# One planner for the whole kernel: the first part of a macaron block ordered by the list scheduler, with smaller units, earlier scores and movable copies

## The chip, the cores and the metric

The kernel runs on one core of a Trainium2 chip. The core has a matrix engine (TensorE, in the profile PE, with its weight loads as PEld), a vector engine (VectorE, DVE), an activation engine (ScalarE, ACT), a general engine (GpSimd, POOL) and a queue engine (SyncE, SP). Each works through its own list of instructions in order and waits for the others by semaphores. SP, ACT and POOL also start transfers (DMA), which 16 DMA engines carry out. Indirect transfers, which scatter rows to addresses held in memory, are started by POOL.

The metric is the device time of one execution in microseconds (us). Lower is better.

## The reference

The input is 8 sequences of 256 tokens of 128 numbers. Three residual steps are computed on it:

```python
x = x + 0.5 * ffn(layernorm(x), router_w, w1, v1, w2, bias)
x = x + attention(layernorm(x), qkv_w, proj_w, proj_b, slopes)
x = x + 0.5 * ffn(layernorm(x), router_w, w1, v1, w2, bias)     # the same weights

def ffn(x, ...):                     # 8 experts, hidden width 352
    scores = softmax(x @ router_w)   # each token goes to its best two experts
    weights, idx = top_k(scores, 2)
    h = gelu(x @ w1[e]) * (x @ v1[e])
    y = h @ w2[e]
    return sum_k(weights[k] * y[idx[k]]) + bias

def attention(x, ...):               # 16 heads of 8, rotary turning of q and k
    s = q @ k.T * 8**-0.5 + min(j - i, 0) * slope[h] * 8
    return softmax(s) @ v @ proj_w.T + proj_b
```

All numbers are 32-bit floats.

## The kernel before

**First part.** The 2048 tokens are four blocks of 512 (two sequences each, four tiles of 128 tokens). For each block `ffn_prep` (line 634) normalises the rows (`ln_stats`, `ln_apply`; one step of the normalisation, a power, runs on POOL), turns them (`ln_turn`) and calls `route` (line 555). `route` multiplies by the router, finds the best two experts, counts with matmuls where each row goes among the rows of its expert, and has POOL scatter the rows to a buffer `xs` in HBM (line 621): one indirect transfer for 128 rows, eight for a block, 32 for a part. `wave` (line 659) makes a table of the 128-row tiles that are sure to be full so far: 8 tiles after two blocks, 16 after three, and all 39 after the fourth. In the last wave SP also writes blank rows behind each expert's last row (`pad`, line 677 to 681), eight transfers whose addresses it loads from the table `t_free`.

**Expert tiles.** The class `Tiles` (line 747) works off the table. For a tile, `load` (line 770) has SP fetch 128 rows into `xr` (10 buffers), `turn_x` transposes them, `weights` copies the expert's first weights to `ws`, `hidden` makes `g` and `v` (Gelu on ACT, product on DVE), and `second` multiplies by the other weights into `y`, scales it into `yo` (4 buffers) and has POOL scatter it to `ys` in HBM (line 836). A part always runs 36 tiles; three more stand behind a branch (`others`). In a step j, y of tile j - 3 comes before g and v of tile j - 1.

**Attention.** It runs in 32 groups n: 8 sequences times four groups of four heads (`group`, line 1009). A group has scores `s` on PE into four PSUM buffers; minima with bias on DVE (`ex`, `least`); Exp on ACT; transposes `eT` on PE; copies `et`, two on ACT and two on DVE; `o` on PE, then `og`, `ogT` and the division. `post1` reads the first part's results back and normalises them, `att_prep` makes q, k and v of a sequence, `after` projects. After every second sequence, `after` routes a block of the second part; the last wave of that part comes after the last block. The second part's expert tiles start when the last scores are done.

**What sets the order.** For attention and the second part an explicit planner, the class `Plan` (line 284), notes every operation with an engine, a duration, a due time and its needs, and `order` (line 351) places them as a list scheduler: at each step it takes the operation that can start first, by smaller due time among those that can start within 0.1 us. The instructions of PE, DVE, ACT and SP are then issued in that order; POOL's others are kept in it too, and its scatters stand behind the POOL operation ahead of them. The first part is not in the planner (`plan = None`, line 403): its instructions stand in the order of the text, and the framework orders each engine. Its loads are issued at the top: x on SP and ACT, weights `wall` on SP, six small tensors on ACT. `attention_constants` (line 171) spreads the preparation of attention over the first part's tiles. `behind` keeps two instructions of an engine in order. Between the parts the branch of `others` separates the two stretches of code.

Of the kernel before, what the change touches and what calls it, by code (L numbers as in the profile page):

```python
# [15 lines left out]
P = 128  # L16
# [21 lines left out]
def full_tiles(blocks):  # L38

    return (2 * TB * blocks - E * (P - 1)) // P  # L40
# [3 lines left out]
def tile_macaron(  # L44
# [30 lines left out]
    xs0 = []  # L75
    for b in range(NBLK):
        t = res.tile([P, TT, D], F32, tag=f"x0_{b}", name=f"x0_{b}")
        (nc.scalar if b % 2 else nc.sync).dma_start(
            t.rearrange("p (s t) d -> p s t d", t=2), xf[:, 2 * b : 2 * b + 2]
        )  # L80
        xs0.append(t)
    rw = const.tile([P, E], F32, name="rw")
    nc.scalar.dma_start(rw, router_w)
    wall = const.tile([P, E, WW], F32, name="wall")
    hb = const.tile([P, D], F32, name="hb")
    pb = const.tile([P, D], F32, name="pb")
    sl = const.tile([P, H], F32, name="sl")
    for e in range(E):
        nc.sync.dma_start(wall[:, e, 0:F], w1[e])
        nc.sync.dma_start(wall[:, e, F : 2 * F], v1[e])  # L90

    nc.vector.memset(wall[:16, :, 2 * F + D :], 0.0)
    for c, cut in enumerate(CUTS):
        skip = 16 if c else 0
        nc.sync.dma_start(
            wall[skip:, :, 2 * F + c * D : 2 * F + (c + 1) * D],
            w2[:, cut + skip : cut + P, :].rearrange("e p d -> p e d"),
        )
    qkvT = const.tile([P, 3 * D], F32, name="qkvT")
    pwT = const.tile([P, D], F32, name="pwT")  # L100
    cs = const.tile([P, 2, 2, 2, HD], F32, name="cs")
    nc.scalar.dma_start(sl, slopes.partition_broadcast(P))
    nc.scalar.dma_start(hb, bias.partition_broadcast(P))
    nc.scalar.dma_start(pb, proj_b.partition_broadcast(P))
    nc.scalar.dma_start(cs, rope.rearrange("(p n) a b d -> p n a b d", n=2))
    nc.scalar.dma_start(qkvT, qkv_wT)
    nc.scalar.dma_start(pwT, proj_wT)


    blank = const.tile([P, SPARE + E, RW], F32, name="blank")  # L110
    ident = const.tile([P, P], F32, name="ident")
    make_identity(nc, ident)
    half = const.tile([P, TT], F32, name="half")
    nc.vector.memset(half, -0.5)
    before = const.tile([P, P], F32, name="before")
    nc.gpsimd.memset(before, 1.0)
    nc.gpsimd.affine_select(
        out=before, in_=before, compare_op=ALU.is_gt, fill=0.0, base=0,
        pattern=[[1, P]], channel_multiplier=-1,
    )  # L120
    ones = const.tile([P, P], F32, name="ones")
    nc.gpsimd.memset(ones, 1.0)

    def counting(shape, pattern, name):
        cf = const.tile(shape, F32, name=name)
        ci = cf.bitcast(I32)
        nc.gpsimd.iota(ci, pattern=pattern, base=0, channel_multiplier=0)
        nc.vector.tensor_copy(cf, ci)
        return cf

    last_wave = NT - full_tiles(NBLK - 1)
    experts = counting([P, E], [[1, E]], "experts")
    regions = counting([P, E], [[REG, E]], "regions")

    rows = []
    for b in range(NBLK):
        t = const.tile([P, 2, TT, RW], F32, tag=f"rows{b}", name=f"rows{b}")
        for k in range(2):
            nc.gpsimd.iota(
                t[:, k, :, D : D + 1].bitcast(I32), pattern=[[SEQ, 2], [1, 2], [0, 1]],  # L140
                base=TOK * k + b * TB, channel_multiplier=2,
            )
        rows.append(t)
    steps128 = counting([P, E, 16], [[0, E], [P, 16]], "steps128")
    tiles = counting([P, last_wave, E], [[1, last_wave], [0, E]], "tiles")
    upto = const.tile([P, E, E], F32, name="upto")
    nc.gpsimd.memset(upto, 1.0)
    nc.gpsimd.affine_select(
        out=upto, in_=upto, compare_op=ALU.is_ge, fill=0.0, base=0,
        pattern=[[1, E], [-1, E]], channel_multiplier=0,  # L150
    )

    mask = const.tile([P, 4], F32, name="mask")

    vpad = [const.tile([P, 2, H, 32], F32, tag=f"vp{i}", name=f"vp{i}") for i in range(3)]


    strip = 3 * P
    alibi = const.tile([P, H, strip], F32, name="alibi")

    def behind(ins, other):

        tc.add_manual_dep(
            ins if isinstance(ins, mybir.Instruction) else ins.ins, other,
            mybir.DependencyInfo(
                mybir.DependencyClass.NoSync, mybir.DependencyReason.DATA
            ),
            reason="in the order of the text",
        )

    def attention_constants(other):


        def late(ins):
            behind(ins, other)

        late(nc.vector.tensor_scalar(hb, hb, 0.5, None, ALU.mult))
        late(nc.vector.tensor_reduce(
            mask, ident.rearrange("p (i j d) -> p j i d", j=4, d=HD), AX.XY, ALU.add
        ))  # L180
        yield
        for b in range(NBLK):
            late(keep(part0, b, xs0[b]))
            yield
        for t in vpad:
            late(nc.vector.memset(t, 0.0))
            late(nc.vector.memset(t[:, :, :, HD : HD + 1], 1.0))
            yield
        di = work.tile([P, 2 * SEQ], F32, tag="yg", name="di", bufs=4)[:, :strip].bitcast(I32)
        nc.gpsimd.iota(  # L190
            di.rearrange("p (a c) -> p a c", c=P), pattern=[[1, 3], [2, P]], base=-1,
            channel_multiplier=-2,
        )
        df = work.tile([P, 2 * SEQ], F32, tag="yg", name="df", bufs=4)[:, :strip]
        late(nc.vector.tensor_scalar(df, di, 0, None, ALU.min))
        yield
        for h in range(H):
            late(nc.vector.tensor_scalar(
                alibi[:, h, :], df, sl[:, h : h + 1], 8.0, ALU.mult, ALU.mult
            ))  # L200
            if h % 2:
                yield

    def run(gen):
        for _ in gen:
            pass


    ENG = mybir.EngineType
    PE, DVE, ACT, POOL, SP = ENG.PE, ENG.DVE, ENG.Activation, ENG.Pool, ENG.SP  # L210

    class Root:


        def __init__(self, make, slot=None, bufs=0, bank=False):
            self.make, self.slot, self.bufs, self.bank = make, slot, bufs, bank
            self.tile = None
            self.ops = []

        def real(self):  # L220
# [63 lines left out]
    class Plan:  # L284
# [7 lines left out]
        def note(self, eng, us, call, reads, writes, lands=0.0):  # L292
# [10 lines left out]
            for late, writing in [(x, False) for x in reads] + [(x, True) for x in writes]:  # L303
                root = late.root
                for other, region, wrote in root.ops:
                    if other is op:
                        continue
                    if root.bank and (other.eng is not eng or wrote != writing):
                        op.needs.add(other)
                    elif (wrote or writing) and meet(region, late.region):  # L310
                        op.needs.add(other)
# [923 lines left out]
```

## Time and profile before

| what | us |
|---|---|
| median of 3 runs | 463.69 (461.45 to 463.88) |
| the profiled execution itself | 498.11 |
| its span, first to last instruction | 496.4 |
| busy: PE / DVE / ACT / POOL | 383.7 / 310.2 / 269.6 / 247.2 |
| first row scatter of the first part begins | 21.5 |
| row scatters of the first part end | 70.9 |
| last y of the first part begins | 147.1 |
| first and last scores (groups 0 and 31) begin | 165.0 and 365.7 |
| last y scatter of the second part begins | 479.1 |

The profile is one execution recorded by the hardware profiler, some 34 us longer than the runs. In its lines an operation is named by line, engine and by what it writes and reads; `L415` and `L422` are the two lines of the helper through which nearly all operations pass, outside (`L415`) and inside the planner (`L422`). "Idle before" is the time for which an engine stood still ahead of an operation, and what ended that; "remote" means that the trace names nobody.

### The profile page before, as it was taken

To read this page: it belongs to the slowest core of one execution; us is meant where nothing else is said; L and a number is where in the kernel's file an instruction comes from. 1 tells how busy PE (TensorE), PEld (TensorE's weight loads), DVE (VectorE), ACT (ScalarE), POOL (GpSimd) and SP (SyncE) were. 2 spreads that over 40 slices of the span, in tenths; PEclk is the share of its full clock that TensorE was granted. 3 is DMA by queue.
4 is the path that set the end of the run, shared out by engine and by line. 5 is a ranking of instruction groups with operands and counts; after the bars stand their busy time and mean duration, and the time that the engine had idled before them with its cause. 6 is when DMAs were issued, how large, how long until landed. Compare 5 with 4: busy or idle time off the path is not lost. (4 is left out here: it accounts for less than half of the span.)

```text
span 496.4 us, 11146 instructions
## 1 busy us (share of the span) xinstructions
PE 383.7 (77%) x3272; PEld 310.6 (63%) x3272; DVE 310.2 (62%) x1300; ACT 269.6 (54%) x671; POOL 247.2 (50%) x324
## 2 busy tenths in 40 slices
PE   0643559999982788998999899788959984999950
PEld 0533449999981555656665566456636974899940
DVE  7332337874432697889888978698856671545514
ACT  2510214554540678888888797578847561445520
POOL 7273564554441136346948895638060546354430
PEclk9999988999996599999999999899997997999985
DMA  7971322222112110000000000010010112222116
GB/s 218 241 148 41 83 81 61 56 71 66 56 32 80 34 44 23 1 1 3 1 17 29 1 2 17 23 34 17 2 43 13 35 55 63 66 72 65 44 52 232
DMA packets 31646, 27.59 MB, mean 56 GB/s; under 512 B 4832, under 2 KB 29408, under 8 KB 31584
## 3 DMA queue, kind: packets, MB, share of 16 engines
q1 hardware_dynamic: 23760, 15.05, 11.7%
q0 software_dynamic: 4352, 8.99, 5.7%
q10 hardware_dynamic: 3472, 2.80, 1.7%
q8 instruction: 29, 0.48, 0.4%
q14 instruction: 33, 0.27, 0.2%
HBM read 14.80 MB, written 12.02 MB: 54 GB/s over the span
## 5 line engine op out<-in xcount | busy, mean ns | idle before, releaser
L422 ACT ACTIVATE ex<-ex,least 128x256 f32<-128x256 f32 x256 | 116.3, 504 | 21.6 <-DVE least L422 21.2
L836 POOL DMA_INDIRECT ys<-yo,xr x72 | 72.7, 1010 | 102.9 <-ACT yo L415 39.9
L422 DVE CUSTOM_DVE_ANT_0 ex<-s,alibi 128x256 f32<-128x256 f32 x256 | 96.0, 418 | 28.7 <-PE s L422 13.3
L621 POOL DMA_INDIRECT xs<-rows,r_at_f x64 | 63.1, 986 | 57.4 <-issue 15.7
L422 PE MATMUL eT<-ident,ex 128*128 128x128 f32 x512 | 78.4, 286 | 12.6 <-DVE et L422 7.5
L422 PEld LDWEIGHTS eT<-ident,ex 128*128 128x128 f32 x512 | 58.5, 145 | 35.2 <-ACT ex L422 24.8
L825 PE MATMUL y<-wall,gs 128*128 x432 | 62.9, 283 | 18.2 <-issue 8.9
L825 PEld LDWEIGHTS y<-wall,gs 128*128 128x128 f32 x432 | 55.4, 196 | 20.8 <-issue 9.6
L795 DVE COPY ws<-wall 128x704 f32 x72 | 38.4, 533 | 14.4 <-issue 7.4
L422 DVE COPY et<-eT 128x512 f32<-128x512 f32 x64 | 43.0, 684 | 2.6 <-remote 1.4
L422 PE MATMUL o<-et,vp 128*32 128x256 f32 x512 | 43.1, 400 | 0.8 <-DVE et L422 0.5
L422 DVE TENSOR_TENSOR gs<-gs,v 128x384 f32<-128x384 f32 x36 | 19.9, 553 | 36.8 <-PE xT L422 19.0
L422 ACT COPY et<-eT 128x512 f32<-128x512 f32 x64 | 36.5, 578 | 8.7 <-PE eT L422 7.6
L422 PE MATMUL s<-kT,qT 32*128 32x256 f32 x512 | 40.6, 419 | 0.6 <-DVE kT L422 0.6
L415 DVE TENSOR_TENSOR gs<-gs,v 128x384 f32<-128x384 f32 x36 | 19.8, 550 | 33.1 <-PE xT L415 14.1
L415 PE MATMUL g<-xTs,ws 128*128 128x128 f32 x216 | 32.1, 288 | 0.0
L422 PE MATMUL g<-xTs,ws 128*128 128x128 f32 x216 | 31.1, 281 | 0.6 <-DVE r_row_f L422 0.5
L415 PE MATMUL v<-xTs,ws 128*128 128x128 f32 x216 | 31.6, 284 | 0.0
L422 POOL TENSOR_SCALAR qT<-qa,mask 128x256 f32<-128x256 f32 x28 | 25.6, 928 | 10.9 <-ACT qa L422 10.8
L422 PEld LDWEIGHTS s<-kT,qT 32*128 32x128 f32 x512 | 25.7, 192 | 7.7 <-issue 4.6
L422 POOL TENSOR_TENSOR t<-qk,cs 128x128 f32<-128x128 f32 (+1 forms) x36 | 18.8, 550 | 23.2 <-ACT qk L422 23.1
L422 PE MATMUL v<-xTs,ws 128*128 128x128 f32 x216 | 30.3, 277 | 0.0
(219 smaller groups left out, 651.2 us busy)
## 6 DMA issues: line engine op xcount, KB each, us to landing
xr<-xs SPq DMA_DIRECT2D x72, 65.0 KB
yg<-ys SPq DMA_DIRECT2D x10, 256.0 KB
wall<-in_w_dram SPq DMA_DIRECT2D x8, 176.0 KB
wall<-in_v_dram SPq DMA_DIRECT2D x8, 176.0 KB
ys<-yo,xr POOLq DMA_INDIRECT x72
xs<-blank SPq DMA_DIRECT2D x16, 65.0 KB
xs<-rows,r_at_f POOLq DMA_INDIRECT x64
yg<-ys ACTq DMA_DIRECT2D x4, 256.0 KB
```

Of the source, the lines that this page charges most:

```text
L415: return f(*[real(x) for x in a], **{n: real(x) for n, x in k.items()})
L422: lambda: f(*[real(x) for x in a], **{n: real(x) for n, x in k.items()}),
L621: nc.gpsimd.indirect_dma_start(out=part.xs, in_=real(rows[b])[:, k, t, :], in_offset=None, out_offset=bass.IndirectOffsetOnAxis(ap=real(at ...
L795: nc.vector.tensor_copy(real(ws), flat[:, bass.ds(w, 2 * F)])
L825: nc.tensor.matmul(real(py), real(hT)[:, c, :], flat[:, bass.ds(w + 2 * F + c * D, D)], start=(c == 0), stop=(c == 2),)
L836: nc.gpsimd.indirect_dma_start(out=self.part.ys, in_=real(yo), in_offset=None, out_offset=bass.IndirectOffsetOnAxis(ap=real(xr)[:, D : D + ...
```

## The change

- The planner orders the whole first part too. Every load, constant, router step and table is noted as an operation with a due time; `plan = None` at the top becomes `plan = Plan()`, and `issue` issues a plan.
- The units of routing are sequences. First part: four units of one sequence (two tiles), then two of two. Second part: three blocks of two sequences, then two single ones. Waves come accordingly: 4, 8, 16 and 39 tiles in the first part, 8, 16, 20 and 39 in the second.
- Small tensors are loaded by SP; ACT loads three of the six pieces of x and the router's weights.
- The counting matmuls of `route` become two: running sums are made on DVE first.
- The eight pads of the second part's last wave are replaced by `no_rows_anywhere`: eight transfers on ACT, one behind every third tile of the first part, that fill all regions of the second part's `xs` with blank rows (17 x 128 rows of 520 bytes each).
- The planner knows engines that are interchangeable for an operation (`either`), Gelu and Exp table loads (1.3 us), and the landing of scatters; for SP it looks 2.6 us ahead.
- In attention, scores and minima are due half a group earlier (`DUE_S`, `DUE_M`); the `et` copies go to ACT or DVE, whichever the planner finds free; `post1` and `att_prep` are due earlier, and the second half of block 0 is prepared by DVE.
- `warm` makes ACT load the table of Exp or Gelu with a one-element operation, and eight matmuls of 512 columns whose result is not used (`idle`) are put at the head of the second plan.

```diff
-def full_tiles(blocks):
-    return (2 * TB * blocks - E * (P - 1)) // P
+def full_tiles(n):
+    return NT if n == NB else max(0, (2 * SEQ * n - E * (P - 1)) // P)
+DUE_S, DUE_M, DUE_E, DUE_T, DUE_C, DUE_V, DUE_G, DUE_O, DUE_I = (
+    -0.5, -0.5, 0.1, 0.9, 0.9, 1.4, 1.4, 1.8, 0.1
+)
...
-                        t = self.room(op, max(t, free[e]))
+                        t = self.room(op, max(t, free[e], landed.get(op.takes_from, 0.0)))
...
-                        soon = min(can)[0] + 0.1
+                        soon = min(can)[0] + (2.6 if e is SP else 0.1)
                         first = min((c for c in can if c[0] <= soon), key=lambda c: c[1:3])
...
+                if op.table not in (None, table):
+                    table = op.table
+                    op.end += 1.3
+                if op.lands_in is not None:
+                    landed[op.lands_in] = max(landed.get(op.lands_in, 0.0), op.end + op.lands)
...
-    plan = None
+    plan = Plan()
...
+    def either(out, in_, act, dve):
+        def copy():
+            (nc.scalar.copy if op.eng is ACT else nc.vector.tensor_copy)(real(out), real(in_))
+        op = plan.note(ANY, act, copy, [in_], [out])
+        op.engines = {ACT: act, DVE: dve}
...
+    UNITS = [(0, 0, 2), (0, 2, 4), (1, 0, 2), (1, 2, 4), (2, 0, 4), (3, 0, 4)]
+    for u, (b, t0, t1) in enumerate(UNITS):
+        (sc if u % 2 else sy).dma_start(
...
+        sy.dma_start(t, given, us=0.4, lands=12.0)
...
+    at(24.0, 0.02)
+    blank = fixed([P, SPARE + E, RW], "blank")
+    gp.memset(blank, 0.0, us=1.8)
...
+    def warm(f):
+        t = new(work, [P, 1], F32, "warm", "warm", 1)
+        sc.activation(t, half[:, 0:1], f, us=0.2)
...
+    def no_rows_anywhere(part, e):
+        region = part.xs[REG * e : REG * (e + 1), :].rearrange("(n p) d -> p n d", p=P)
+        own = blank[:, SPARE + e, :].unsqueeze(1).to_broadcast([P, REG // P, RW])
+        op = sc.dma_start(region, own, us=0.5, lands=8.0)
...
+        ve.tensor_copy(sums[:, 1, :], both[:, 0, :], us=0.12)
+        for t in range(1, n):
+            ve.tensor_tensor(sums[:, t + 1, :], sums[:, t, :], both[:, t, :], ALU.add, us=0.12)
+        with together(1.0):
             te.matmul(pp, before, both, start=True, stop=False)
-            for t in range(TT):
-                n = TT - t
-                te.matmul(
-                    pp[:, t + 1 :, :], ones, both[:, t : t + 1, :].to_broadcast([P, n, E]),
-                    start=False, stop=(n == 1),
-                )
+            te.matmul(pp, ones, sums, start=False, stop=True)
...
-        if last:
+        if last and i == 0:
             free = new(work, [P, E], I32, "t_free", f"t_free{i}", 1)
...
+    for u, (b, t0, t1) in enumerate(UNITS):
+        early = u < 4
+        at(4.0 + 3.0 * u, 0.1)
+        ffn_prep(part0, b, t0, t1 - t0, xs0[b][:, t0:t1, :], sc)
+        n = 2 * b + t1 // 2
...
+        more = full_tiles(n) - len(part0.table)
+        if more > 0:
+            wave(part0, more, n == NB)
+    at(200.0, 0.1)
+    plan.needs = [part0.tabled]
+    attention_constants()
...
+    plan.needs = part0.exps
+    at(20.0)
+    warm(AF.Gelu)
...
+    while True:
+        at(36.0 + 2.1 * work0.j)
+        if not work0.step():
+            break
+    part1 = Part(1)
+    for e in range(E):
+        at(60.0)
+        plan.needs = [work0.turned[2 + 3 * e]]
+        no_rows_anywhere(part1, e)
...
-        plan.due = n
+        plan.due = n + DUE_S
         with together(1.15) as op:
...
-            if i < 2:
-                sc.copy(et, pt, us=0.58)
-            else:
-                ve.tensor_copy(et, pt, us=0.69)
+            plan.due = n + DUE_C + DUE_I * i
+            either(et, pt, 0.58, 0.69)
...
+        if blk + 1 < NBLK:
+            if s % 2 == 0:
+                return
+            t0, n = 0, TT
+        else:
+            n = 2
+        ffn_prep(part1, blk, t0, n, x2[blk][:, t0 : t0 + n, :], sc if s + 1 == NB else gp)
...
+    at(-20.0)
+    idle = new(ps_b, [P, TB], F32, "B", "idle")
+    with together(6.5):
+        for _ in range(8):
+            te.matmul(idle, ident, wall[:, 0, 0:TB], start=True, stop=True)
+    at(-9.0)
     post1(0, ve, slice(0, 1))
+    warm(AF.Exp)
...
-            post1(0, gp, slice(1, 2))
+            post1(0, ve, slice(1, 2))
...
-                plan.due, plan.pace = 8.0 * b - 6, 0.12
+                plan.due, plan.pace = 8.0 * b - 8, 0.12
                 post1(b, gp)
...
-            plan.due, plan.pace = n + 1.2, 0.08
+            plan.due, plan.pace = n + 0.2, 0.08
             att_prep(s + 1, gp)
```

## The prediction

> **What bounds the kernel now.** I read the busy time by stage first (columns: stretch and its length, busy time and instructions of PE, PE's loads, DVE, ACT, POOL, granted clock, DMA share, GB/s).
>
> ```profile
> 21.50:52.30 30.80, 11.96 (x53) 10.88 (x53) 11.61 (x94) 4.47 (x11) 19.06 (x20) 1.00 0.53 112
> 52.30:76.50 24.20, 14.22 (x74) 13.30 (x75) 7.38 (x37) 5.22 (x13) 14.07 (x15) 0.88 0.24 70
> 76.50:149.00 72.50, 70.50 (x622) 69.69 (x620) 43.46 (x97) 36.48 (x97) 34.18 (x34) 0.99 0.20 57
> 149.00:165.00 16.00, 4.82 (x10) 2.25 (x11) 5.72 (x22) 2.44 (x8) 2.13 (x3) 0.61 0.20 62
> 165.00:365.70 200.70, 180.42 (x1700) 120.48 (x1700) 167.66 (x792) 159.97 (x391) 118.15 (x175) 0.97 0.06 17
> 365.70:419.00 53.30, 37.79 (x307) 32.52 (x307) 28.80 (x117) 24.81 (x60) 22.39 (x23) 0.90 0.14 42
> ```
>
> Expert tiles are PE-bound from 76.5 us on: one per 2.12 us, 19 PE instructions of 0.11 us. Before that PE is mostly idle: tiles wait for rows, and rows for POOL, which issues 32 row scatters 1.265 us apart (0.96 busy, 0.30 issue). Attention is mixed, 6.47 us per group; from 365.7 to 419 PE idles again, waiting for the last block's rows.
>
> The second view is the timeline, because the profiled execution (498.1 us; span 496.4) is 34.4 us above the median of the runs, 463.7:
>
> ```profile
> 21.47 1.19 POOL L621 DMA_INDIRECT xs<-rows,r_at_f  x1 [9.23 <-ACT xnT L415]
> ...
> 43.65 0.19 DVE L415 TENSOR_TENSOR both<-r_pick_f 128x32 f32<-128x32 f32 x1 [3.92 <-remote]
> ...
> 71.56 0.49 ACT L415 ACTIVATE gs<-g 128x384 f32<-128x384 f32 x1 [5.45 <-remote]
> ...
> 371.98 0.42 DVE L422 CUSTOM_DVE_ANT_0 ex<-s,alibi 128x256 f32<-128x256 f32 x1 [4.80 <-remote]
> ```
>
> The instructions of line 677 alone (durations as least/median/most ns):
>
> ```profile
> L677 SPq TENSOR_LOAD <-t_free x16: 3/252/626, 60.7 to 422.8; - x16
> ```
>
> About five scatters into a row burst, DVE, ACT and PE stop together and resume when the burst ends, while POOL keeps its 1.265 us. They wait for nothing that the trace names, and SP's register loads (median 252 ns) are recorded with as little as 3 ns[...]. I take these stops for an effect of recording. Working the chain forward without them, row scatters end at 62.0 instead of 70.9 us, y(4), whose yo buffer waits for the first y scatter, runs at 63.5, and the last y, 31 tiles on, at 129.4 instead of 147.1 (17.7); groups 22 and 23 took 8.0 and 10.6 us instead of 6.3 (6); the stop at 367 cost 5.2, the one at 412 some 6. Together 35, about the 34.4: the timed runs don't have them, so I don't count their removal.
>
> The third view is waits in steady attention, 191.4 to 304.9 us (total us, times, longest):
>
> ```profile
> DVE ex L422 <- ACT et L422: 8.3, 5, 2.3
> DVE ex L422 <- PE s L422: 7.0, 6, 1.5
> ```
>
> DVE, the busier of the two vector engines there (94.2 of 113.5 us), loses 15.3 us in 18 groups to late scores and to copies on ACT.
>
> [...]
>
> **The change, part by part.**
>
> *First scatter.* Now at 21.47, 17.5 us after x is there (3.93). With two-tile units and x, router weight alone on ACT's queue, these go: DVE's 2.5 us between the end of the first power (6.5) and its use (8.96), behind other blocks' statistics; 0.84 us of ACT, whose table load starts only at 9.45 after nine DMA issues; two of four normalisations and block 1's first (1.2); the copy of rows ahead of xnT (0.5); half the router matmuls (8 of 1.88 us: 0.94), half of max and index (1.31: 0.65), counting matmuls (2.3 for ten, four remain: 1.4, less 0.24 for the two new adds), 0.45 of POOL start. Sum 8.2: first scatter at 13.3.
>
> *Row scatters.* Same 32, each unit ready (3 us apart) before POOL is through the one ahead: 13.3 + 40.5 + 1.9 (blank, now between them) = 55.7. In the runs before: 21.5 + 40.5 = 62.0.
>
> *Tiles.* First wave needs 12 scatters instead of 16: 13.3 + 15.2 = 28.5, landed 30.7, loaded 33, PE from 35; Gelu waits for the sixth Exp, about 35 too. Row scatters go ahead of y scatters, and yo has 4 buffers, so y(4) waits for 55.7 + about 3 = 58.5; meanwhile the planner can put g and v of tiles up to 9 (10 xr buffers) ahead: 10 x 1.44 + 4 x 0.67 = 17 us of PE work. Left: 36 x 2.125 - 17 = 59.5, so the last y is near 118.5 to 119, against 129.4. **-10.5**. If the work ahead isn't ordered so, y(35) is at 58.5 + 31 x 2.125 = 124.4: -5. If rows and y scatters interleave ideally, -14.
>
> *Fills.* Eight ACT DMAs of 2176 rows of 520 B replace eight pads of the second part. The trace has none as big. Bounds: an unhindered issue is 0.33 to 0.5 us; two of 896 rows[...] held SP 4.90 us, so 2176 rows would hold ACT 4.90 / 2 x 2176 / 896 = 5.95 us. They come every third tile (6.4 us)[...]. ACT is busy 36.5 of 72.5 us in tiles, which covers 1 us per tile; without cover every us over that delays xTs, gs and yo, and PE behind them. I take **+1.5** for all eight (bounds 0 and +40). The pads themselves (8 x 1.15 us on SP) end before the last rows land: nothing.
>
> *Part to part.* The eight idle matmuls of 512 columns keep the clock up. The 384-column ones were 0.64 us apart at half clock, so 0.43 each for 16 at full: 6.8 us, from 150.5 to 157.3, just when the first transpose is ready (157.4). They save the half clock on the chain: transpose 0.3, qkv 0.6, qkT 0.6, first scores 1.5 (2.69 against 1.15): **-3**. Bounds -4; +6 if PE is at half clock already.
>
> *Attention.* Scores and maxima half a group sooner, copies to the freer engine, preparation sooner. Upper bound: the whole wait for s and half of that for et, (7.0 + 4.15) / 18 x 32 = -20. Lower: 0, or +5 if transposes and copies come late and exps wait for their buffers. I take a third of the upper bound, **-7**, because the ring from scores to copies stays.
>
> *Tail.* Sequences 6 and 7 become separate units: 20 tiles instead of 16 are known before the last one, 4 x 2.12 = 8.5 us of PE work; the last unit has 4 scatters instead of 8 (-5.1) and half the router (-2.7). PE ran 85 instructions of 0.11 us in 400 to 420, so 10.6 us idle, of which some 9 remain in the runs (out of work at 407.7, next tile at 416.7, both shifted for the stop at 367). Rows at 408 against work until 416 close it: **-9** (bounds -4, when DVE's extra unit and wave of 6 us aren't hidden, and -11). After that the chain that ended last, one y per 2.12 us, the four reads and the sums, is unchanged.
>
> **The sum.** 498.1 (profiled) - 34.4 (recording) = 463.7; -10.5 + 1.5 - 3 - 7 - 9 = -28: **435.7 us**. In a profile of it the bursts are longer, so it should show 455 to 485 us.
>
> **Rivals.** *POOL and the greedy order keep most of it*: y scatters wait as now (-5), attention the same (0), tail -4, clock -2: 453. For it: POOL's 68 scatters take 86 us either way, and 83% busy DVE leaves little. Against it: PE's idle time in three stages is plain. *The fills hold ACT*: in place, in tiles 2 to 23, at 5.95 us less 1 of cover, 8 x 4.95 = 40 instead of 1.5: 474, slower. It decides from 28 / 8 = 3.5 us of delay per fill, a hold of 4.5 us. For it: SP's 2.45 us for 896 rows.[...] *The planner orders as the old schedule did and nothing moves*: 463; against it, units and waves differ by construction.
>
> **How the numbers follow.** The case above 0.67 (its own range 424 to 447), the small gain 0.18 (447 to 461), nothing 0.04, slower 0.11. An interval of 8 in 10 reaches down to 421 (upper bounds of attention and tail together) and up to 458. A measurement here tells 0.5%, 2.3 us, from no change: faster 0.85, same 0.04, slower 0.11.
>
> **What would show it.** First row scatter of POOL near 13 us; 12 scatters before the first load of xr; y(35) some 10 us sooner than now once recording stops are taken off; eight xs<-blank DMAs on ACT with short holds; stage between parts at clock 1; group interval near 6.2; in the tail PE without the gap at 405 to 420. It is wrong if fills show holds of 4 us, if PE stands before y(4) to y(10) with g and v not ahead, or if group intervals don't fall; and in size if the stops are in the timed runs as well.

## The result, and the profile after

The changed kernel takes 466.04 us (median of seven, 464.62 to 468.47), the kernel before 461.45 us (459.98 to 463.88): ratio 1.010, interval 1.006 to 1.014. It is 1% slower. Its profiled execution takes 466.5 us, its span is 464.8.

The kernel before took 459.7 to 461.5 us on record and in three of the five later comparisons and 500 us in the other two, where every run of it was so long and the traces have the stops of its first profile, so each kernel is compared with the kernel before of its own comparison.

"After" stands for the changed kernel and "before" for the kernel before; in lines of after, `L317` is the helper through which nearly all operations pass, and `L342` the copy that either engine may take. The busy time of after by stage (columns: stretch and its length, busy time and instructions of PE, PE's loads, DVE, ACT, POOL, granted clock, DMA share, GB/s):

```profile
60.90:76.50 15.60, 11.29 (x84) 10.49 (x84) 8.81 (x24) 4.36 (x13) 5.53 (x7) 0.88 0.87 168
76.50:123.00 46.50, 35.62 (x256) 34.17 (x256) 23.28 (x51) 14.84 (x41) 15.07 (x15) 0.86 0.89 160
123.00:150.50 27.50, 27.50 (x249) 27.50 (x249) 13.38 (x25) 14.37 (x38) 12.58 (x13) 1.00 0.44 92
150.50:170.45 19.95, 14.38 (x52) 7.50 (x51) 6.42 (x24) 5.53 (x14) 4.31 (x5) 0.87 0.19 59
170.45:350.25 179.80, 170.56 (x1659) 117.56 (x1659) 159.06 (x789) 162.63 (x405) 111.34 (x165) 0.97 0.06 17
```

The tile stage, which before was full from 76.5 us on, is full only from 123 on. Until then PE has gaps and falls below full clock, and the DMA engines are 0.87 to 0.89 busy (0.20 in the stage of before). Attention is faster than forecast: 31 groups in 179.8 us, 5.80 each, against a forecast near 6.2 and 6.47 in the profile of before, which has stops in it.

PE's first instruction after each long gap between 60 and 125 us, from the timeline of after:

```profile
73.97 1.65 PE L909 MATMUL y<-wall,gs 128*128 x6 [3.23 <-ACT yo L317]
81.45 0.71 PE L317 MATMUL xT<-ident,xr 128*128 128x128 f32 x2 [1.99 <-DMA xr<-xs]
...
101.51 0.47 PE L317 MATMUL xT<-ident,xr 128*128 128x128 f32 x1 [5.08 <-DMA xr<-xs]
121.41 0.33 PE L317 MATMUL xT<-ident,xr 128*128 128x128 f32 x1 [2.63 <-DMA xr<-xs]
```

Three of the four end with the load of a tile's rows; the first ends with `yo` on ACT, which stood still ahead of a fill (below). POOL's timeline:

```profile
15.87 1.19 POOL L699 DMA_INDIRECT xs<-rows,r_at_f  x1 [5.74 <-DVE r_sm_f L317]
...
26.50 1.04 POOL L317 TENSOR_TENSOR rs_f<-nt_f,half 128x4 f32<-128x4 f32 x1 [1.88 <-DVE r_row_f L317]
...
61.22 1.11 POOL L920 DMA_INDIRECT ys<-yo,xr  x1 [0.30 <-issue]
```

The first row scatter comes 5.6 us sooner than before (8.2 forecast), the row scatters end at 61 instead of the forecast 55.7: POOL waits for a unit and does two powers of later units between scatters. SP's register loads for the pads (durations least/median/most ns) have none of the 3 ns records of before:

```profile
L757 SPq TENSOR_LOAD <-t_free x8: 267/850/907, 60.5 to 86.8; - x8
```

The last y of the first part starts at 153.2, the first scores at 170.45, the last scores at 350.25. The issue of a fill takes ACT 0.38 to 0.45 us each, as in its timeline:

```profile
61.75 0.39 ACTq L317 DMA_DIRECT2D xs<-blank  x1
67.18 0.27 ACT L317 COPY xTs<-xT 128x128 f32<-128x128 f32 x1 [0.34 <-PE xT L317]
72.58 0.38 ACTq L317 DMA_DIRECT2D xs<-blank  x1
73.00 0.49 ACT L317 ACTIVATE gs<-g 128x384 f32<-128x384 f32 x1 [5.55 <-DMA xs<-blank]
```

One exception: ahead of the third fill ACT does nothing from 67.45 to 72.58, 5.1 us, with the next gs behind it, and that is PE's first gap above. In the four later traces of kernels with whole fills and without stops, ACT stands at the same place for 1.7 to 3.0 us. The second fill comes 1.6 us behind ACT's last instruction, the other six at once.

### The profile page after: what moved, and what is told of

It reads as the page before. It is cut to its first block, busy times and chain, and to the rows that moved or that the text cites. A ratio compares the mean times of both kernels' runs of the same rounds, so it can differ in the third digit from the quotient of the medians.

```text
span 464.8 us, 11188 instructions
## 1 busy us (share of the span) xinstructions
PE 381.6 (82%) x3252; PEld 310.3 (67%) x3252; DVE 323.0 (70%) x1411; ACT 277.0 (60%) x698; POOL 247.6 (53%) x328
## 3 DMA queue, kind: packets, MB, share of 16 engines
q10 hardware_dynamic: 20160, 11.42, 12.5%
## 4 chain that ended last, share of the span: by engine, by line
DVE 22%; POOL 22%; PE 18%; issue 17%; DMA 12%; ACT 5%; SPq 1%; DVEq 1%; POOLq 1%; ACTq 0%
POOL ys L920 10%; DVE ex L317 6%; PE eT L317 4%; PE s L317 3%; DMA xs<-rows,r_at_f 3%; DMA ys<-yo,xr 3%; POOL qT L317 2%; ACT ex L317 2%; DMA xr<-xs 2%; DMA yg<-ys 2%; POOL xs L699 2%; POOL rows L317 2%; PE o L317 2%; DVE et L342 2%; PE v L317 2%
## 5 line engine op out<-in xcount | busy, mean ns | idle before, releaser
L317 ACT ACTIVATE ex<-ex,least 128x256 f32<-128x256 f32 x256 | 114.0, 507 | 6.7 <-DVE least L317 6.6
L317 DVE CUSTOM_DVE_ANT_0 ex<-s,alibi 128x256 f32<-128x256 f32 x256 | 92.0, 418 | 11.7 <-PE s L317 10.3
L317 PE MATMUL eT<-ident,ex 128*128 128x128 f32 x512 | 75.3, 282 | 4.9 <-ACT et L342 1.9
L317 DVE TENSOR_TENSOR gs<-gs,v 128x384 f32<-128x384 f32 x72 | 39.7, 552 | 56.3 <-PE xT L317 32.4
L317 PEld LDWEIGHTS eT<-ident,ex 128*128 128x128 f32 x512 | 58.1, 143 | 24.4 <-issue 8.5
L317 PE MATMUL g<-xTs,ws 128*128 128x128 f32 x432 | 63.8, 286 | 5.7 <-DVE ws L879 5.4
L317 PE MATMUL v<-xTs,ws 128*128 128x128 f32 x432 | 63.3, 285 | 0.0
L317 PEld LDWEIGHTS g<-xTs,ws 128*128 128x128 f32 x432 | 57.2, 202 | 6.5 <-DVE ws L879 5.1
L317 PEld LDWEIGHTS v<-xTs,ws 128*128 128x128 f32 x432 | 57.3, 202 | 0.0
L317 ACT ACTIVATE gs<-g 128x384 f32<-128x384 f32 x72 | 35.4, 492 | 35.5 <-PE g L317 27.5
L317 ACT ACTIVATE yo<-y,xr 128x128 f32<-128x128 f32 x72 | 26.5, 368 | 43.0 <-PE y L909 38.7
L342 ACT COPY et<-eT 128x512 f32<-128x512 f32 x80 | 45.1, 585 | 6.4 <-PE eT L317 5.5
L317 PE MATMUL s<-kT,qT 32*128 32x256 f32 x512 | 41.9, 427 | 0.6 <-DVE kT L317 0.6
L317 PE MATMUL o<-et,vp 128*32 128x256 f32 x512 | 36.8, 388 | 1.4 <-DVE os L317 1.3
L317 ACT COPY xTs<-xT 128x128 f32<-128x128 f32 x72 | 18.9, 267 | 29.6 <-PE xT L317 29.5
L342 DVE COPY et<-eT 128x512 f32<-128x512 f32 x48 | 32.3, 682 | 3.2 <-PE eT L317 3.0
L317 POOL TENSOR_SCALAR qT<-qa,mask 128x256 f32<-128x256 f32 x28 | 26.2, 951 | 14.8 <-ACT qa L317 14.8
```

Source lines behind the costliest of these rows:

```text
L317: lambda: f(*[real(x) for x in a], **{n: real(x) for n, x in k.items()}),
L342: (nc.scalar.copy if op.eng is ACT else nc.vector.tensor_copy)(real(out), real(in_))
```

## The experiments

The theory: the fills occupy the DMA engines, and row loads, pads and scatters of the first part wait in line with them. The rival: the new order is slow in itself. For the gains that hid the loss the question was which edit brings them.

### The stops, once more

The kernel before, unchanged.

> The kernel before, profiled a second time, to test the step of the prediction that took 34.4 us of its first profile for an effect of recording. If the stops come from recording and are not in the timed runs, a second profile has either the same stops at about the same places (span near 496) or none (span near 462), while the timed run stays at 460 to 464. If the stops belong to the kernel, its timed run would have to show them too, and then a time near 496. With no stops in it, the worked-forward figures can be read off: row scatters end at 62, the last y of the first part at 129, the first scores near 147.

500.07 us, so the second case came, a time near 496, and not 460 to 464; the ten runs beside it took 497.8 to 501.7. The stops are at the same places, SP's register loads have 6 ns as their least. So they are not an accident of one profile, and on that chip they are part of the time. Where the kernel before takes 461 us they are absent: see the attention edits alone, below, whose first part is that of before. What causes them isn't shown by any run.

### The fills left out, the fills moved, the idle matmuls left out

```
# shortened
-    for e in range(E):                          # both kernels
-        plan.needs = [work0.turned[2 + 3 * e]]
-        no_rows_anywhere(part1, e)
# left out: the pads of the second part come back
-        if last and i == 0:
+        if last:
# moved: in the loop over groups n
+        if n < E:
+            plan.due = n + 0.3
+            no_rows_anywhere(part1, n)
```

> The changed kernel without its eight fills; the second part gets eight pads on SP's queue after its last routing, as in the kernel before. Theory A (the traffic of the fills, 9 MB in packets of 520 B, holds up row loads, pads and scatters of the first part): last y near 120 to 128 instead of 150, 438 to 448 us. Theory B (the new order itself is slow in the first part, whatever the fills do): last y stays near 150, 464 to 470 us.

> The changed kernel with the eight fills moved out of the first part: one in each of the first eight groups of attention, where the DMA engines are idle (0.1 busy). Theory A: as without fills, and two or three us better since the last part needs no pads: 436 to 447 us. Theory B: 464 to 468 us. If an issue of a fill holds ACT[...], 8 x 4 us come back in attention: 470 us or more.

The third kernel is the changed one without the group of eight matmuls named idle.

> The changed kernel without the eight matmuls of 512 columns ahead of attention. In its trace they stand in the stage between the parts, and the clock falls to half nevertheless (165 to 179). If they delay the first transposes (they hold PE when the first rows are ready): 461 to 464 us. If they keep PE at full clock for the chain from transposes to first scores as forecast (3 us): 468 to 470 us. If neither: 465 to 467 us.

Against 500.04 us: 483.05 without fills (ratio 0.964, 0.961 to 0.968), 481.42 with the fills in attention (0.959, 0.952 to 0.966), 492.88 without idle matmuls (0.984, 0.980 to 0.988). The changed kernel itself wasn't run there. If the third kernel stands for it, the fills cost about 10 us here, and in attention nothing that shows. The last y starts at 145.2 us without fills and at 142.0 with the fills in attention, against 153.0 in the third kernel: sooner, as the theory has it, but not at the 120 to 128 that was expected, since all three traces have the stops. The expected times were for 461 us of the kernel before. For the idle matmuls the third run settles nothing.

### The changed kernel again, and the attention edits alone and undone

```
# shortened; attention edits alone, in the kernel before (undone in the changed one: the reverse)
-        plan.due = n                              # scores
+        plan.due = n - 0.5
-            plan.due = n + 0.1 + 0.1 * i          # minima
+                plan.due = n - 0.5 + 0.1 * i
-            sc.copy if i < 2 else ve.tensor_copy  # et
+            either(et, pt, 0.58, 0.69)
-            post1(0, gp, slice(1, 2))
+            post1(0, ve, slice(1, 2))
-    8.0 * b - 6 ... n + 1.2                       # preparation
+    8.0 * b - 8 ... n + 0.2
```

> The changed kernel itself, on a chip on which the kernel before takes 500 us as in its first profile. If the ratio on record (1.010) holds wherever the kernels run: 505 us against 500. If the changed kernel has fewer of the stops that the profile of before shows, its ratio is lower here: without the idle matmuls it took 493 against 500, so 490 to 496 against 500 (0.98 to 0.99), and the fills cost 8 to 13 us here.

> The kernel before with the attention edits alone: new due times of scores, maxima, exps; copies of et to either engine; preparation of blocks and sequences one or two groups sooner. If attention gains what the trace of after shows (5.80 us per group against 6.3 to 6.5): 15 to 20 us less than before, ratio 0.96 to 0.97. If it gains the 7 us of the prediction: 0.985. If the gain in after comes from other things (other rows on POOL, an earlier or later start): 0.995 to 1.005.

> The changed kernel with the attention edits undone (old due times, two copies on each engine, old preparation times). The mirror of the run before it: 15 to 20 us above the changed kernel if the edits are worth that, 7 us if the prediction's size is right, 0 to 2 us if nothing hangs on them. If the two don't mirror each other, the greedy order of the parts isn't additive.

Against 461.43 us: the changed kernel 456.03 (0.986, 0.983 to 0.990), the attention edits alone 442.37 (0.960, 0.955 to 0.964), the changed kernel without them 476.61 (1.034, 1.029 to 1.039). Alone they take off 19.1 us, undone they cost 20.6: they are worth 19 to 21 us in both kernels. Everything else in the change costs 14 to 15 us here. The expectation for the changed kernel was made for 500 us of the kernel before, which it didn't take here. That this comparison has the changed kernel below the one before and the record above it lies mostly in the first part: its last y starts at 143.8 here and at 153.2 on record, for the same program. Why isn't shown.

With the attention edits undone, the waits of DVE and ACT in attention (190 to 305 us; total us, times, longest) are

```profile
ACT ex L317 <- DVE least L317: 12.5, 26, 1.9
...
DVE ex L317 <- ACT et L317: 7.6, 5, 1.6
DVE ex L317 <- PE s L317: 7.6, 8, 1.5
```

and in the changed kernel (trace of the record, 201.8 to 310.3 us),

```profile
DVE ex L317 <- PE s L317: 4.6, 8, 1.0
PEld eT L317 <- ACT et L342: 3.8, 8, 0.9
```

The wait of minima (`ex` on DVE; the expectations call them maxima) for copies on ACT is gone from the list, that of exps for minima is down from 12.5 to 1.2 us, that for scores is 4.6 instead of 7.6.

The kernel with the attention edits alone also shows the first part of before without stops (POOL):

```profile
61.38 1.28 POOL L640 DMA_INDIRECT xs<-rows,r_at_f  x1 [0.30 <-issue]
62.97 1.20 POOL L855 DMA_INDIRECT ys<-yo,xr  x1 [0.30 <-issue]
```

The last row scatter ends at 62.7 (62.0 worked forward in the prediction), y(4) starts at 63.2 (63.5), the last y at 132.9 (129.4), the first scores at 150.8.

### One unit in the tail

```
-        if blk + 1 < NBLK:
-            if s % 2 == 0: return
-            t0, n = 0, TT
-        else:
-            n = 2
+        if s % 2 == 0: return
+        t0, n = 0, TT
```

> The changed kernel with sequences 6 and 7 as one unit of four tiles again, as in the kernel before. The prediction's step: 9 us slower than the changed kernel. From the trace of after (scores of the last group to the end 114.5 us): 4 to 5 us slower. If the second unit's extra work on DVE and POOL takes the gain back: within 1.5 us.

461.96 us, but the four runs lie at 453.7 and 461.6 to 462.3, so the medians don't tell what the unit is worth. From the last scores to the end it takes 116.8 us, the changed kernel 114.0: 2.8, in one trace of each. Of the 8.2 us between the two traces 3.9 lie in the first part, which this edit doesn't touch (last y 147.7 against 143.8): with the fills in it that part varies from run to run.

### Half the fills, late fills, late fills without idle matmuls

```
-        region = part.xs[REG * e : REG * (e + 1), :]   # 17 x 128 rows
+        region = part.xs[REG * e : REG * e + 8 * P, :] # 8 x 128 rows
...
```

The half fills leave 1152 rows of each region unwritten. Late fills are the edit above; the last kernel is that without the idle matmuls.

> The changed kernel, as the reference for the three beside it; it stood at 1.010 of the kernel before on record and at 0.986 in a later comparison, where the DMA engines moved 180 to 195 GB/s during the fills instead of 160. Nothing but a figure between 0.985 and 1.012 is expected.

> The changed kernel with every fill cut from 2176 to 1024 rows (the rest of the regions stays unwritten, which this input never reads); the order of every engine is the same. Traffic theory: the fills' bytes are the cost, so a bit over half of it goes: 6 to 12 us less than the changed kernel beside it, last y of the first part 5 to 12 us sooner. If the eight issues on ACT or their place in the order are the cost: within 1.5 us of the changed kernel.

> The eight fills in the first eight groups of attention instead of the first part, beside the changed kernel and half the fills on one chip. Traffic theory: 11 to 22 us less than the changed kernel, 438 to 446 us if the kernel before takes 461; the last y of the first part at 126 to 133. If the new order of the first part is worth what the prediction gave it (last y at 119): below 436 us.

> As the run ahead of it, without the eight idle matmuls. If they delay the first transposes: 2 to 5 us less than with them. If they keep the clock for the chain to the first scores (3 us in the prediction): 3 us more. If neither: within 1.5 us.

Against 459.68 us: changed kernel 454.81 (0.989, 0.984 to 0.994), half fills 439.83 (0.957, 0.952 to 0.963), late fills 438.51 (0.954, 0.949 to 0.959), without idle matmuls 439.35 (0.954, 0.949 to 0.959). The fills cost 16.3 us, and taking half of them away gives 15.0 of it back, more than expected. The instructions of PE, DVE, POOL and SP stand in the same order in both traces, and the eight issues on ACT remain, so it is traffic, not order; and it isn't proportional. ACT's stand ahead of the third fill is gone too, so this run doesn't separate that stand from the later landings. Half fills, stretches of 25 us:

```profile
75.00:100.00 25.00, 24.66 (x220) 24.36 (x219) 18.89 (x43) 12.58 (x35) 12.44 (x13) 1.00 0.56 149
100.00:125.00 25.00, 25.00 (x227) 25.00 (x226) 12.98 (x24) 13.31 (x36) 11.19 (x13) 1.00 0.29 79
```

At a DMA share of 0.56 PE is full; at 0.87 to 0.89, above, it isn't. With late fills:

```profile
59.78:76.50 16.72, 16.39 (x145) 15.94 (x144) 14.92 (x37) 7.98 (x23) 10.68 (x11) 1.00 0.31 88
76.50:129.56 53.06, 51.83 (x463) 51.45 (x461) 31.12 (x64) 26.91 (x72) 24.73 (x26) 1.00 0.21 58
```

Most of how the loss comes about is seen on SP. Its timeline in after (record):

```profile
61.19 6.65 SPq L761 DMA_DIRECT2D xs<-blank  x5
73.42 9.86 SPq L853 DMA_DIRECT2D xr<-xs  x6
84.64 3.53 SPq L761 DMA_DIRECT2D xs<-blank  x3
92.85 41.56 SPq L853 DMA_DIRECT2D xr<-xs  x17
```

and with late fills:

```profile
55.70 5.16 SPq L762 DMA_DIRECT2D xs<-blank  x5
63.55 8.62 SPq L854 DMA_DIRECT2D xr<-xs  x6
72.94 2.60 SPq L762 DMA_DIRECT2D xs<-blank  x3
77.46 6.20 SPq L854 DMA_DIRECT2D xr<-xs  x6
```

Between the eighth pad and the first load of the last wave, which needs every pad landed, lie 4.7 us (88.2 to 92.85) instead of 1.9 (75.5 to 77.46). The DMA issues of after, with the time to landing in us,

```profile
xs<-blank SPq DMA_DIRECT2D x8, 65.0 KB, 5.7
```

and of late fills:

```profile
xs<-blank ACTq DMA_DIRECT2D x8, 1105.0 KB, 7.7
...
xs<-blank SPq DMA_DIRECT2D x8, 65.0 KB, 1.8
```

A pad of 128 rows lands in 5.7 us beside the fills and in 1.8 without (4.6 to 8.7 in the four later traces with whole fills and such a time, 3.7 with half). Everything that SP's queue holds behind such a landing is later each time, 9.9 us at the loads from 73.42 on and 15.4 us at those from 92.85 on. SP's own waits for landings of y scatters and pads in the first part (us in total, times, longest), in after

```profile
SPq L853 <- DMA ys<-yo,xr: 20.2, 5, 9.8
SPq L853 <- DMA xs<-blank: 7.9, 2, 4.4
```

and with late fills:

```profile
SPq L854 <- DMA ys<-yo,xr: 15.1, 16, 1.9
SPq L854 <- DMA xs<-blank: 0.7, 1, 0.7
```

The longest, 9.8 us, ends at 113.9, when a y scatter begun at 105.2 has landed; the load at 114.00 stood behind it. The loads at 73.42, 92.85 and 114.00, each the first behind such a wait, are those of tiles 10, 16 and 23 (counted from 0), and it is their rows that PE waits for in the gaps that end at 81.45, 101.51 and 121.41.

The idle matmuls: from the last y scatter to the first scores, late fills without them, then with them:

```profile
131.22:147.37 16.15, 4.82 (x10) 2.25 (x11) 5.73 (x22) 3.93 (x10) 2.40 (x3) 0.52 0.20 65
```

```profile
129.56:144.42 14.86, 10.69 (x27) 4.63 (x27) 5.73 (x22) 3.94 (x10) 2.40 (x3) 0.86 0.22 72
```

With them the granted clock of that stage is 0.86 instead of 0.52, and the stage is 1.3 us shorter; in the medians, 0.8 us, it can't be told from nothing.

### Bytes or packets, and units of four tiles

```
# shortened; real fills in attention; in the first part, at their old place:
+        region = unread[REG * e : REG * e + n * P, :].rearrange("(p n) d -> p (n d)", p=P)
+        sc.dma_start(region, blank.rearrange("p n d -> p (n d)"))   # n = 15
# units, with late fills:
-    UNITS = [(0,0,2),(0,2,4),(1,0,2),(1,2,4),(2,0,4),(3,0,4)]
+    UNITS = [(0,0,4),(1,0,4),(2,0,4),(3,0,4)]
```

> The kernel with the real fills in attention (0.954 of the kernel before), and in the first part, at the place of the old fills, eight writes of 1920 rows to a tensor that nobody reads, laid out so that each partition writes 7.8 KB in one stretch: 8.0 MB as 1024 stretches instead of 9.05 MB as 17408 rows of 520 B. If the cost of the fills is bytes: 0.88 of 16 us come back, ratio 0.98 to 0.99. If it is the number of small packets: 0 to 4 us, ratio 0.952 to 0.963.

> The kernel with the fills in attention, and the first part routed in four units of four tiles instead of six (two tiles each for blocks 0 and 1). The prediction put the first scatter 8.2 us sooner and the last y 10.5 us sooner for the new first part; 5 us of it are there in the kernel with late fills. If the small units bring those 5: first scatter 3 to 6 us later, last y 3 to 6 us later, ratio 0.961 to 0.968. If the order by the planner brings them, whatever the units: 0.951 to 0.958.

Against 499.87 us: 482.14 (0.963, 0.958 to 0.969) and 481.49 (0.962, 0.958 to 0.967); late fills had 0.959 in the other comparison of this kind. So 8.0 MB in the first part cost 1 to 2 us if they are written in long stretches, less than the intervals tell from nothing, where the rows of 520 B cost about 10 on a chip with the same stops; the 0.98 that bytes would give lies outside the interval. The two writes differ in more than length: a fill repeats one row of `blank` in each partition, a stretch reads all of it and goes to another tensor. The windows of that kernel:

```profile
75.00:100.00 25.00, 24.34 (x208) 23.34 (x208) 20.32 (x51) 10.90 (x32) 9.71 (x10) 1.00 0.54 186
100.00:125.00 25.00, 25.00 (x225) 24.87 (x224) 15.05 (x32) 12.96 (x36) 12.03 (x13) 1.00 0.58 193
```

More GB/s than in after (160), at two thirds of the DMA share, and that share is the one that half the fills have, which cost little too. The time of a row follows from ACT's queue, which held 2624 packets without fills (1.5% of 16 x 485.9 us) and 20160 with them: 11.2% of 16 x 452.5 us beside late fills, 40 ns of an engine for each of the 17536 more; 12.5% of 16 x 464.8 us on record, 46 ns; with half the fills 10944 in 5.2% of 16 x 437.3 us, 30 ns. So a row took longer with whole fills than with half. A long stretch of 7.8 KB took 322 ns (mean of the 1024 packet records of that size). The whole fills are 17408 x 40 / 16 = 43 us of all 16 engines (50 on record), half the fills 15, the long stretches 21.

Small units hardly count: with units of four the first scatter is at 18.3 instead of 15.9, but the row scatters end 1 us sooner and the last y comes 1.4 us later (single traces, late fills from the other comparison).

### The two attention edits apart

Each alone in the kernel before, with the preparation as it was.

> The kernel before with only the due times of scores and maxima half a group sooner; copies fixed, preparation as before. All attention edits together took 19 us off (0.960). If each edit removes its own wait, scores sooner are worth the wait for s, 7.0 of 18 groups by 32: 12 us, ratio 0.973. If the whole gain hangs on the due times: 0.957 to 0.965. If on the copies: 0.99 to 1.0.

> The kernel before with only the copies of et given to whichever of ACT and DVE is free in the plan; due times and preparation as before. If each edit removes its own wait: half of the 8.3 us for et by 32 / 18, 7 us, ratio 0.984. If the whole gain hangs on the copies: 0.957 to 0.965. If on the due times: 0.99 to 1.0. What neither this nor the run ahead of it explains of the 19 us belongs to the earlier preparation or to the edits working only together.

Against 499.87 us: 495.66 (0.988, 0.982 to 0.994) and 493.78 (0.987, 0.982 to 0.991). From first to last scores they take 7.5 and 6.3 us less than the second trace of the kernel before, and all edits together, in the first trace of late fills, 7.2 (6.23 against 6.46 per group): with the stops nothing adds up. So the two went once more:

> The kernel before with only the due times of scores and maxima half a group sooner, a second comparison: in the first one the kernel before took 500 us and its attention was cut by stops of all engines that the chips with 461 us don't show. Alone it took 7.5 us from the first to the last scores there, of 7.7 for all attention edits. Where the kernel before takes 461 us, all edits together took 19 us off. If the two edits add up there: 8 to 12 us, ratio 0.974 to 0.983. If one alone brings nearly all, as with the stops: 0.957 to 0.965.

> The kernel before with only the copies of et to either engine, the same comparison: 6.4 us of attention alone with the stops. If the two edits add up where there are no stops: 7 to 11 us, ratio 0.976 to 0.985. If the copies alone bring nearly all: 0.957 to 0.965. If nothing without the due times: 0.99 to 1.0.

Against 461.29 us: 454.67 (0.986, 0.978 to 0.993) and 456.77 (0.987, 0.979 to 0.994), that is 6.6 and 4.5 us in the medians, less than the 8 to 12 and 7 to 11 that were expected, and neither brings nearly all. No trace of before is without stops; if the 19.1 us all lie between the first and the last scores, its attention lasts 176.3 + 19.1 = 195.4 us, an estimate; with the due times alone it lasts 188.1, with the copies alone 190.7, with all edits 176.3. The two give 12 us (11 in the medians) if they add up; the other 7 or 8 belong to the earlier preparation or to the edits working together, which no run separates.

## Why the prediction was wrong

Forecast 436, measured 466; the range (421 to 458) missed it and the sign was wrong. What was measured for each term, without the stops: the attention edits alone against late fills for first part, transition and tail, in single traces.

| term | forecast | measured |
| --- | --- | --- |
| first part without fills (last y) | -10.5 | -5.0 (132.9 to 127.9) |
| fills | +1.5 | +16.3 in runs; +25.3 on record (last y 127.9 to 153.2) |
| part to part | -3 | -1.5 (18.0 to 16.5 from last y to scores) |
| attention | -7 | -19.1 |
| tail | -9 | -1.2 (114.8 to 113.6); -2.8 by one unit |

The runs close the sum better: late fills are 21 us below the kernel before, of which 19.1 are attention, so the three other gains are 2 to 4 us in medians (the traces' 7.6 compare the longest run of one with the shortest of the other). Late fills lie 22.9 us below the kernel before of the record, and the changed kernel on record 27.5 us above late fills (466.0 against 438.5): -22.9 + 27.5 = +4.6, across two comparisons. Of the 27.5 the runs beside each other show 16.3; why the fills cost some 10 us more on record stays open. There a row took 46 ns instead of 40, and ACT stood 5.1 us instead of 1.7.

**Fills.** The step that failed: it took +1.5 us for the issues and put the traffic at nothing. The price of an issue was right (0.4 us), and the hold of 5.95 us that it had as a bound nearly came once on record (5.1 us at the third fill; what held ACT there isn't shown). That such holds would mostly stay away was the author's estimate, which no trace of before showed. The DMA engines' time, which the fills share with row loads and pads, got no price. Loads went on beside the fills (SP issued six in the 9.86 us from 73.42), but pads landed in 5.7 us instead of 1.8. The profile of before allowed an estimate: ACT's queue moved 3472 packets in 1.7% of 16 x 496.4 us, 39 ns each; 17408 rows are 42 us of all 16 engines (43 to 50 measured), laid over a stage of 72 us whose loads and scatters already took 0.2 of them and were waited for. Its bounds (0 to +40) held the value; the point taken stood at their lower end. The rival "the fills hold ACT" had the right part and a time, 474, nearer than 436, but that is in part luck: it counted eight holds of 5.95 us, and ACT was held once.

**First part.** The second alternative of that step (-5) is about what came, by other means: the last y starts at 131.1 to 134.2 in the three traces without stops that have the old first part, at 127.9 and 129.6 in the two with late fills. PE's work isn't out of order: with late fills it is busy from 50.2 on almost without a gap, and the last y starts at 127.9, 36.6 tiles of 2.12 us later. The start failed: PE was to work from 35 on, but the twelfth row scatter ended at 34.8 instead of 28.5, the first g came at 42.0, and then

```profile
50.22 1.65 PE L317 MATMUL g<-xTs,ws 128*128 128x128 f32 x6 [4.74 <-DVE ws L880]
```

the copy of the second tile's weights stands on DVE behind the routing of the last unit and a wave's table.

**Part to part.** Sign right, size half: of the 16.2 us of that stage without the idle matmuls PE is busy 4.8, so most of the chain lies elsewhere. In the profile of before the granted clock is 0.50 from 155 to 167 us, and the first scores take 2.69 us. On record the idle matmuls run from 154.9 to 162.0; the clock is 1.00 from 153 to 165, then 0.50 to 0.51 until 177, and the first scores take 2.69 us there too.

**Attention.** The upper bound of the step (-20) was reached. The third of it that was taken had as its only reason that the ring from scores to copies stays; that reason failed, for the waits on that ring shrank or went with the edits. The trace of before had 15.3 us of the two waits in 18 groups, 27 in 32, and 19 us were gained; the two edits alone bring 11 to 12 of these.

**Tail.** The 10.6 us that PE stood idle at 400 to 420 in the profile of before were mostly a stop, of which the step kept 9 as real. The prediction counted that stop twice, for it had "the one at 412 some 6" among those that the runs don't have. The profile shows

```profile
410.32 0.91 PE L825 MATMUL y<-wall,gs 128*128 x6 [2.74 <-issue]
418.76 1.65 PE L825 MATMUL y<-wall,gs 128*128 x6 [6.14 <-issue]
```

and the trace of the attention edits alone, without stops,

```profile
365.69 0.91 PE L844 MATMUL y<-wall,gs 128*128 x6 [2.77 <-DVE gs L433]
```

The first gap is the same, the second is not there; from y(10) to y(15) it takes 12.4 us instead of 10.6. So there was little to gain: the tail lasts 113.5 to 114.8 us in the three traces with the old tail and 113.6 and 112.9 in the two with late fills.

**The stops.** That the runs on record don't have them was right: the worked-forward times hold within 3.5 us. That they come from recording was not shown and falls as it was put: on two chips every run of the kernel before takes 500 us, though runs elsewhere, recorded as well, take 461. And a profile of after was to show 455 to 485 us; it showed 466.5, but with no stop in it.

## What to carry to other kernels

Price a background transfer in DMA engine time, packets by ns per packet over 16 engines (30 to 46 ns for the rows of 520 B here), and lay it over the stage where it runs: where the sum with the stage's own traffic came to 0.87 to 0.89 of the engines here, pads landed in 5.7 us instead of 1.8, and along the chain of landings the delays added up (SP's loads 9.9, then 15.4 us later). Move such a transfer to a stage that waits for few loads, or write it in long stretches: the same fills in attention bring the DMA share there to 0.32, with 0.9 or more in three of the four slices of 10.9 us from 152 to 196 us, and cost nothing that shows (attention 177.0 us against 176.3 without them), and late fills (438.5 us, 0.954 of before) beat both kernels. When a change bundles gains and a loss, take each part alone before judging it by the sum.

## What the runs showed of the hardware that was not expected

- Rows of 520 B written to DRAM took 40 ns of an engine each (13 GB/s per engine) with whole fills and 30 ns (17 GB/s) with half, stretches of 7.8 KB 322 ns (24 GB/s). So rows of 520 B reach 0.54 to 0.72 of what long stretches do.
- The cost of background traffic isn't proportional to its amount, and the DMA share alone doesn't set it: at 0.56 PE stayed full (24.7 of 25 us), at 0.89 on record it was busy 35.6 of 46.5 us. In the trace of the changed kernel beside half the fills it was busy 19.7 of 25 us at 0.79 (75 to 100 us) and 24.1 of 25 at 0.88 (100 to 125).
- The first part of the same program ended at 143.8 to 153.2 us in different comparisons with the fills in it: the changed kernel stands at 1.010 of the kernel before on record and at 0.986 and 0.989 later, late fills at 0.954 and 0.959.
- On two chips the kernel before takes some 38 us longer in every run, and the traces taken there show PE, DVE and ACT stop together during bursts of scatters; the cause is open.
